# Reordered softmaxes, weight loads and first FFN tiles in a float32 gated cross-attention block on one core

## The chip, the cores and the metric

The kernel runs on one core of a Trainium2 chip. The metric is the device time of one execution in microseconds; lower is better. Three runs of the kernel before gave 1563.82, 1565.23 and 1566.9 us; their median is 1565.23 us.

## The reference

For 32 sequences of 64 tokens of width 512 the kernel computes a cross-attention with 32 heads of width 128 and then a linear layer with a low-rank adapter, both added to the tokens through a gate:

```python
x = x + jnp.tanh(g_xattn[0]) * xattn(_layernorm(x), ctx, mask, bias, Wq, Wk, Wv, Wo)
x = x + jnp.tanh(g_ffn[0]) * ffn(_layernorm(x), weight, bias, lora_A, lora_B, starts)

# xattn: per head
score = einsum('bqhd,bkhd->bhqk', q, k) / sqrt(128) + position_bias    # masked keys: -inf
ctx = einsum('bhqk,bkhd->bqhd', softmax(score), v)                      # then ctx @ Wo
# ffn
y = x @ weight.T + bias + lora(x)
```

All data are float32. Products of the projections are made from operands that are split into a high and a low part, three matmuls for one.

## The kernel before, in words

**Halves and pairs.** The 2048 tokens are worked through in two halves of 1024 (index p). A half has two stages. Stage A (function stage_a) projects the context to keys and values and writes them to device memory. Then the function attention goes through the 32 heads as 16 pairs (n from 0 to 15). The second half ends with the FFN of all tokens, in four chunks of 512 tokens (c from 0 to 3) of four tiles (t).

**One pair.** q_unit(n) makes the queries of a pair with seven products of split blocks (line 352; the block weights are named p1 to p7). score(n) makes the scores, and on VectorE (DVE) adds the bias and takes the maximum (lines 775 and 777); GpSimd (POOL) subtracts it (778), ScalarE (ACT) takes the exponential (787, for pair 0 783). The generator normed sums the row on DVE and multiplies by the reciprocal on POOL (797 to 800). Then the probabilities must be turned: a DVE transpose in 32 x 32 blocks writes a tile tp (811), and eight small ACT copies for each head place its blocks into the tile pts that the value products read (808). pv(n) multiplies by the values (891), in four PSUM groups of two heads i and two column halves c, and splits the result into ch on ACT and cl on DVE (894, 895). oproj(n) multiplies these with the pair's output weights, eight tiles of tokens, and adds each to acc on DVE (925). The weights of queries and of the output come raw from device memory (fetch, line 259), are split by eight steps of prep (305) or two of prep_o (906), on ACT and POOL, and are used then.

**What sets the order.** Each engine executes its instructions in the order in which the Python code issues them. Side work is written as generators in the list streams. beat() (64) advances each of them by one step and is called after every product of a unit, every score, every value group and every output tile. drain(g) runs a generator to its end at once. So the order on ACT, DVE, POOL and SyncE's queue of DMAs (SP) is that of streams at each beat. The sequence of the pairs is written out by hand in run (939). Pairs 0 and 1 go singly, then the loop of line 1005 takes two pairs a pass, from a = 4 to 14, and lines 1020 to 1035 end the half.

**Around the change.** Pair 0's softmax is both(normed(0), first_turned()): row sums of both heads first, then head 0 turned through tp and eight ACT copies, and head 1 turned by eight small DVE transposes right into pts. Pairs 14 and 15 are last_turned() (847): sums and products of pair 14, then, head by head, those of pair 15 and the turn of pair 14, then the turns of pair 15 beside copies, two memsets of a second tile of probabilities, and the rest of the copies. Raw query weights are fetched into one buffer, r0: at the start of odd query units, and after a drain of the even ones' split (lines 998 and 1006). The values of a pair have one buffer (res[3]) of 1 MB, so v of pair 15 is loaded when pv(14) has ended. start_o(14), the split of output 14's weights, begins in line 1024. In the second half the stream ffn_weights (1078) first splits the FFN weights and then normalizes the first four tiles of tokens (ffn_norm); the four transposes and splits of these (ffn_tile, lines 1104 to 1109) stand between the first four tiles of output 13 (between, 1209), and fill (1214) then runs chunk 0 of the FFN. In the first half, fill makes a part of the second half's first keys. ffn_lora(c) is the first user of a chunk's split tiles.

Of the kernel before, what the change touches and what calls it, by code (L numbers as in the profile page):

```python
# [9 lines left out]
F32 = mybir.dt.float32  # L10
# [7 lines left out]
P = 128  # L18
# [25 lines left out]
def flamingo_block(ctx: ExitStack, tc: tile.TileContext, x, xT, ctxT, bias, mask, gx, gf,  # L44
# [257 lines left out]
    PREP = (("s3", "hp1"), ("s2", "lp1", "hp7"), ("s1", "lp7", "hp6"), ("s4", "lp6", "hp5"),  # L302
            ("lp5", "hp2"), ("lp2", "hp4"), ("lp4", "hp3"), ("lp3",))

    def prep(kind, n, eng, wait=0, at=0):
        for _ in range(wait if at == 0 else 0):
            yield
        do = pair_blocks(kind, n, eng)
        for k, ops in enumerate(PREP):
            if at and k == at:  # L310
                for _ in range(wait):
                    yield
            do(*ops)
            yield

    def prep_plain(n, eng, only=None):
# [394 lines left out]
    def attention(p, res, rest):  # L711
# [6 lines left out]
        def load_v(n):  # L718
            b["v", n] = big(res[3], [P, NT, 256], F32, f"v{p}_{n}")
            nc.sync.dma_start(out=b["v", n], in_=vd[p][n // 2][:, :, n % 2 * 256:(n % 2 + 1) * 256])  # L720

        def load_bias(n):
            for i in range(2):
# [31 lines left out]
        def enter_late():  # L755
            nonlocal acc_t, ch, cl
            ch = big(rest[0], [P, 2, TP], F32R, f"ch{p}")
            cl = big(rest[1], [P, 2, TP], F32R, f"cl{p}")
            acc_t = [big(res[5 + i], [P, 4, 512], F32, f"acc{p}_{i}") for i in range(2)]
            acc.extend(acc_t[t // 4][:, t % 4, :] for t in range(NT))  # L760
            fetch("o", p * NPR, "r1")
            for t in range(NT):
                nc.sync.dma_start(out=acc[t], in_=x[p * NT + t])

        acc_t = sm = ch = cl = None
        acc, pts = [], []
# [62 lines left out]
                yield  # L829


        def first_turned():
            n = 0
            tp = rows.tile([P, NT, S], F32, tag="row", name=f"tp{p}_{n}")
            turn(tp, n, 0)
            yield
            for k, q in enumerate(quads):
                copy(nc.scalar.copy, n, 0, tp, *q)
                copy(nc.vector.transpose, n, 1, sm[0][:, 1], *q)
                if k % 3 == 2:  # L840
                    yield
            load_bias(2)
            b["m", 2] = bias_mask(2)
            streams.append(b["m", 2])


        def last_turned():
            n = NPR - 2
            z = kqp.tile([P, 2, NT, S], F32, tag="kq", name=f"tz{p}")
            tp = [rows.tile([P, NT, S], F32, tag="row", name=f"tp{p}_{n}_{i}") for i in range(2)]  # L850
            pts.append(big(res[1], [P, 2, NT, P], F32, f"pz{p}"))
            yield from normed(n, 0)
            for i, _ in enumerate(normed(n + 1, 0)):
                turn(tp[i], n, i)
                yield
            todo = [(n, i, q) for i in range(2) for q in quads]

            def copies(k):
                for m, i, q in todo[:k]:
                    copy(nc.scalar.copy, m, i, tp[i] if m == n else z[:, i], *q)  # L860
                del todo[:k]

            for i in range(2):
                turn(z[:, i], n + 1, i)
                copies(3)
                yield
            for h in range(2):
                nc.vector.memset(pts[1][h * S:(h + 1) * S, :, :, (1 - h) * S:(2 - h) * S], 0.0)
                copies(3)
                yield  # L870
            copies(4)

            def rest():
                todo.extend((n + 1, i, q) for i in range(2) for q in quads)
                while todo:
                    copies(4)
                    yield
            b["s", n + 1] = rest()
            streams.append(b["s", n + 1])
# [4 lines left out]

        def pv(n, cs=(0, 1)):
            drain(b["s", n])
            for c in cs:
                for i in range(2):
                    ps = psum(f"po{p}_{n}_{i}_{c}")
                    for t in range(4):  # L890
                        nc.tensor.matmul(ps[:, t * P:(t + 1) * P], b["v", n][:, c * 4 + t, i * P:(i + 1) * P],  # L891
                                         pts[n > NPR - 2][:, i, c * 4 + t, :], start=True, stop=True)
                    sl = slice(c * 512, (c + 1) * 512)
                    nc.scalar.copy(ch[:, i, sl], ps)  # L894
                    nc.vector.tensor_tensor(cl[:, i, sl], ps, ch[:, i, sl].bitcast(F32), ALU.subtract)  # L895
                    beat()
# [42 lines left out]
        def run(xq, prefetch, before_last, last_unit, fill, freed, last, between=None):  # L939
            qb = {}  # L940

            def start_q(n, *a):
                qb[n] = prep("q", p * NPR + n, *a)
                streams.append(qb[n])

            def q_unit(n):
                g = p * NPR + n
                drain(qb.get(n))
                if n == 0:
                    start_q(1, nc.vector, 2)  # L950
                elif n == NPR - 1:
                    before_last()
                elif n % 2:
                    fetch("q", g + 1, "r0")
                else:
                    start_q(n + 1, nc.gpsimd)
                qT[n] = kqp.tile([P, 2, TP], F32, tag="kq", name=f"qT{g}")
                end = unit(wt[("q", g)], xq, None, k_dst(qT[n]), f"q{g}", tuple(carry))
                carry.clear()
                end()  # L960
                if n == NPR - 1:
                    last_unit()
                elif n % 2 and n > 1:
                    start_q(n + 1, nc.gpsimd)

            def score(*ns):
                for n in ns:
# [2 lines left out]
                    for i in range(2):  # L970
                        scores(n, i, qT[n], b["k", n])
                for n in ns:
                    if n + 2 < NPR:
                        load_k(n + 2)
                n = ns[0]
                if n == 0:
                    b["s", n] = both(normed(n, 0), first_turned())
# [55 lines left out]
            oproj(n - 1, range(4, NT))  # L1033
            pv(n, (1,))
            last(lambda t: oproj(n, range(t, t + 1)), acc)

# [41 lines left out]
    def ffn_weights(tags):  # L1078
        wf = [big(tags[i], [P, KT, 512], F32R, f"wf{i}") for i in range(2)]
        ffn_w.update(wf=wf, tags=tags)  # L1080
        for kt in range(KT):
            split(ffn_w["raw"][:, kt, :], wf[0][:, kt, :], wf[1][:, kt, :], nc.gpsimd)
            yield
# [9 lines left out]
        ffn_w["xn"] = big(tags[6], [P, 4, D], F32, "xn")  # L1093
        for t in range(4):
            ffn_norm(0, t)
            yield

    def ffn_norm(c, t):
        mv = mv2[:, c * 4:(c + 1) * 4, :]
# [63 lines left out]
    for p in range(NPH):  # L1163
# [39 lines left out]
        else:  # L1203
# [88 lines left out]
```

## Time and profile before

| what | us |
|---|---|
| median of three runs | 1565.23 |
| the profiled execution, its own time | 1568.15 |
| its span, first to last instruction | 1566.4 |
| TensorE matmul (PE) busy in the span | 1531.0 |
| weight load (PEld) | 1287.6 |
| POOL, DVE, ACT busy | 1020.6, 963.9, 724.9 |

The profiled execution's own time is its span and 1.75 us around it. Times in views of the profile count from the span's start. A row of a timeline is: start, length, engine, line, operation, output <- inputs, count, and in brackets the idle time before it and what ended it. A row of waits is: who waited for what: total in us, times, longest. Tiles are named without their buffer numbers: po the value product, pt and pz the turned probabilities, v the values, wo the output weights, rawq the raw query weights, wsq the sums in their split, fa the split FFN tiles, xn the normalized tokens. The two halves' attention runs from about 311 to 754 us and from 1053 to 1514; the FFN's chunk 0 lies inside the second, from 1448 to 1473.

### The profile page before, as it was taken

To read this page: it belongs to the slowest core of one execution; us is meant where nothing else is said; L and a number is where in the kernel's file an instruction comes from. 1 tells how busy PE (TensorE), PEld (TensorE's weight loads), DVE (VectorE), ACT (ScalarE), POOL (GpSimd) and SP (SyncE) were. 2 spreads that over 40 slices of the span, in tenths; PEclk is the share of its full clock that TensorE was granted. 3 is DMA by queue.
4 is the path that set the end of the run, shared out by engine and by line. 5 is a ranking of instruction groups with operands and counts; after the bars stand their busy time and mean duration, and the time that the engine had idled before them with its cause. 6 is when DMAs were issued, how large, how long until landed. Compare 5 with 4: busy or idle time off the path is not lost.

```text
span 1566.4 us, 25095 instructions
## 1 busy us (share of the span) xinstructions
PE 1531.0 (98%) x9000; PEld 1287.6 (82%) x9000; DVE 963.9 (62%) x1609; ACT 724.9 (46%) x1594; POOL 1020.6 (65%) x1128
## 2 busy tenths in 40 slices
PE   9999999999999999998999999999999999999898
PEld 7888888878788888886888888887878888888677
DVE  5665554385576656665686557448556665767664
ACT  6344233444564566456344323344466456645511
POOL 3898478866666666662589757886666666676110
PEclk9999999999999999999999999999999999999999
DMA  5754545474244344431565454547324344434111
GB/s 210 261 194 159 199 163 177 148 293 135 95 148 163 133 177 158 152 109 68 196 245 204 152 186 167 191 148 276 136 94 162 148 139 171 168 143 129 48 34 67
DMA packets 111070, 248.50 MB, mean 159 GB/s; under 512 B 10241, under 2 KB 44033, under 8 KB 106850
## 3 DMA queue, kind: packets, MB, share of 16 engines
q1 hardware_dynamic: 110658, 246.38, 44.3%
q8 instruction: 71, 1.16, 0.3%
q10 hardware_dynamic: 288, 0.52, 0.1%
q14 instruction: 53, 0.43, 0.1%
HBM read 173.45 MB, written 73.42 MB: 158 GB/s over the span
## 4 chain that ended last, share of the span: by engine, by line
PE 87%; POOL 4%; DVE 3%; DMA 2%; issue 2%; ACT 2%; SPq 0%; DVEq 0%; POOLq 0%; ACTq 0%
PE pa L98 18%; PE po L891 7%; PE pzv L98 6%; PE pvv L98 6%; PE pxv L98 6%; PE pzk L98 5%; PE pvk L98 5%; PE pxk L98 5%; PE pxq L98 5%; PE pzq L98 5%; PE pvq L98 5%; PE ps L773 3%; PE pf L98 3%; PE pyv L98 3%; PE ppk L98 2%; PE pyk L98 2%
## 5 line engine op out<-in xcount | busy, mean ns | idle before, releaser
L98 PE MATMUL pa<-wo,ch 128*128 128x512 f32 x1024 | 320.1, 393 | 2.1 <-POOL wo L90 1.6
L98 PEld LDWEIGHTS pa<-wo,ch 128*128 128x128 f32 x1024 | 190.8, 188 | 43.2 <-POOL wo L90 2.6
L925 DVE TENSOR_TENSOR acc<-pa,acc 128x512 f32<-128x512 f32 x256 | 173.0, 682 | 73.8 <-PE pa L98 73.1
L808 ACT COPY pt<-tp 32x256 f32<-32x256 f32 x464 | 187.2, 403 | 67.4 <-DVE tp L811 56.5
L98 PE MATMUL pa<-wo,cl 128*128 128x512 f32 x512 | 199.8, 390 | 0.0
L731 POOL TENSOR_TENSOR sm<-sm,madd 128x512 f32<-128x512 f32 x60 | 76.9, 1291 | 127.3 <-DMA sm<-bias 127.3
L895 DVE TENSOR_TENSOR cl<-po,ch 128x512 fp32r<-128x512 f32 x128 | 87.4, 691 | 78.5 <-ACT ch L894 78.4
L891 PEld LDWEIGHTS po<-pt,v 128*128 128x128 f32 x960 | 112.3, 192 | 14.9 <-ACT pt L808 12.5
L891 PE MATMUL po<-pt,v 128*128 128x128 f32 x960 | 113.9, 276 | 10.7 <-ACT pt L808 10.7
L98 PEld LDWEIGHTS pa<-wo,cl 128*128 128x128 f32 x512 | 96.2, 188 | 20.3
L800 POOL TENSOR_TENSOR sm<-sm,r 128x512 f32<-128x512 f32 x64 | 67.0, 1048 | 70.4 <-DVE r L799 68.9
L90 POOL TENSOR_TENSOR wo<-rawo,wo 128x512 fp32r<-128x512 f32 x64 | 81.4, 1295 | 46.9 <-ACT wo L89 46.8
L778 POOL TENSOR_TENSOR sm<-sm,mx 128x512 f32<-128x512 f32 x64 | 67.2, 1050 | 63.0 <-DVE mx L777 63.0
L894 ACT CAST ch<-po 128x512 fp32r<-128x512 f32 x128 | 74.7, 590 | 60.1 <-PE po L891 58.3
L354 DVE TENSOR_TENSOR vt<-pvv,vt 128x512 f32<-128x512 f32 x64 | 44.1, 689 | 93.6 <-PE pvv L98 93.5
L354 DVE TENSOR_TENSOR qT<-pvq,qT 128x512 f32<-128x512 f32 x64 | 44.2, 690 | 69.3 <-PE pvq L98 69.1
L354 DVE TENSOR_TENSOR kT<-pvk,kT 128x512 f32<-128x512 f32 x56 | 38.5, 688 | 67.0 <-PE pvk L98 67.0
L376 ACT COPY vt<-pxv 128x512 f32<-128x512 f32 x32 | 18.9, 589 | 130.9 <-PE pxv L98 130.9
L787 ACT ACTIVATE sm<-sm 128x512 f32<-128x512 f32 x60 | 38.0, 633 | 64.7 <-POOL sm L778 64.7
L354 DVE TENSOR_TENSOR qT<-pzq,qT 128x512 f32<-128x512 f32 x64 | 44.2, 690 | 36.7 <-PE pzq L98 36.4
L773 PE MATMUL ps<-kB,qT 128*64 128x64 f32 x2048 | 64.1, 223 | 0.3 <-DVE qT L354 0.3
L773 PEld LDWEIGHTS ps<-kB,qT 128*64 128x64 f32 x2048 | 61.3, 138 | 3.7 <-issue 1.4
(984 smaller groups left out, 3737.1 us busy)
## 6 DMA issues: line engine op xcount, KB each, us to landing
kd<-kT SPq DMA_DIRECT2D x64, 512.0 KB, 3.4
vd<-vt SPq DMA_DIRECT2D x128, 256.0 KB, 2.3
kB<-kd SPq DMA_DIRECT2D x32, 1024.0 KB, 9.8
v<-vd SPq DMA_DIRECT2D x32, 1024.0 KB, 7.9
rawq<-wq SPq DMA_DIRECT2D x32, 512.0 KB, 8.7
sm<-bias SPq DMA_DIRECT2D x64, 256.0 KB, 7.0
rawo<-wo SPq DMA_DIRECT2D x32, 512.0 KB, 3.6
rawk<-wk SPq DMA_DIRECT2D x31, 512.0 KB, 5.4
```

The source lines that it names most:

```text
L90: eng.tensor_tensor(lo, raw, hi.bitcast(F32), ALU.subtract)
L98: nc.tensor.matmul(ps, a, b, start=start and i == 0, stop=stop and i == 3 * n - 1, skip_group_check=True)
L354: nc.vector.tensor_tensor(o, ps, i, ALU.add)
L731: nc.gpsimd.tensor_tensor(t, t, masks[p][0], ALU.add)
L773: nc.tensor.matmul(ps[h * S:(h + 1) * S, t, :], qT[:, i, tok], kT[:, i, tok], start=True, stop=True)
L778: nc.gpsimd.tensor_tensor(s, s, mx.unsqueeze(2).to_broadcast([P, NT, S]), ALU.subtract)
L800: nc.gpsimd.tensor_tensor(t, t, r.unsqueeze(2).to_broadcast([P, NT, S]), ALU.mult)
L808: f(pts[n > NPR - 2][dst, i, :, src], of[src, :, ki * 32:(ki + 1) * 32])
L891: nc.tensor.matmul(ps[:, t * P:(t + 1) * P], b["v", n][:, c * 4 + t, i * P:(i + 1) * P], pts[n > NPR - 2][:, i, c * 4 + t, :], start=True, ...
L894: nc.scalar.copy(ch[:, i, sl], ps)
L895: nc.vector.tensor_tensor(cl[:, i, sl], ps, ch[:, i, sl].bitcast(F32), ALU.subtract)
L925: nc.vector.tensor_tensor(acc[t], ps, acc[t], ALU.add)
```

## The change

- prep takes a function, then, that its last step calls. start_q gives it the fetch of the next pair's raw query weights; the fetches after drains and at the start of odd units go, and so do these drains. Query 2's split starts before pv(0), query 4's with query unit 3, not after it.
- Pair 0's softmax (first_softmax) goes head by head: sum and turn of head 0, then sum and turn of head 1. Head 1 has both ways: its first four blocks by DVE transposes, the other four through a second tp and ACT copies. pv(0) takes both column halves of head 0 first. Output 0's split starts after five products of query unit 1, no longer ahead of them.
- The loads of acc leave two per beat in a stream (load_acc), followed by the keys of pair 2.
- Pairs 14 and 15: pair 14 is turned right after its own products; then come the sums of pair 15, its turns, and the memsets in the rest.
- pv(14) loads v of pair 15 by halves into the same tile, each when its half of pair 14 is used up.
- start_o(14) comes ahead of output 13, and output 14 gives six tiles, not four, ahead of pv(15).
- The FFN stream starts with the four norms; the four FFN tiles stand between the last four tiles of output 12; the first norm of chunk 1 is in fill.

```diff
-    def prep(kind, n, eng, wait=0, at=0):
+    def prep(kind, n, eng, wait=0, at=0, then=None):
...
             do(*ops)
+            if then and k == len(PREP) - 1:
+                then()
             yield
...
+        def load_v(n, t=None, cs=None):
+            b["v", n] = t or big(res[3], [P, NT, 256], F32, f"v{p}_{n}")
+            for sl in [slice(c * 4, c * 4 + 4) for c in cs] if cs else [slice(0, NT)]:
+                nc.sync.dma_start(out=b["v", n][:, sl], in_=vd[p][n // 2][:, sl, n % 2 * 256:(n % 2 + 1) * 256])
...
+        def load_acc():
             for t in range(NT):
                 nc.sync.dma_start(out=acc[t], in_=x[p * NT + t])
+                if t % 2:
+                    yield
+            load_k(2)
...
-        def first_turned():
+        def first_softmax():
             n = 0
+            tp = [rows.tile([P, NT, S], F32, tag="row", name=f"tp{p}_{n}_{i}") for i in range(2)]
+            norm = normed(n, 0)
+            next(norm)
+            yield
+            turn(tp[0], n, 0)
+            yield
+            next(norm)
+            for q in quads[:4]:
+                copy(nc.scalar.copy, n, 0, tp[0], *q)
+            yield
+            for q in quads[4:]:
+                copy(nc.scalar.copy, n, 0, tp[0], *q)
+            turn(tp[1], n, 1)
+            yield
+            for k in (0, 2):
+                for q in quads[k:k + 2]:
+                    copy(nc.vector.transpose, n, 1, sm[0][:, 1], *q)
+                for q in quads[4 + k:6 + k]:
+                    copy(nc.scalar.copy, n, 1, tp[1], *q)
+                yield
...
             yield from normed(n, 0)
-            for i, _ in enumerate(normed(n + 1, 0)):
+            for i in range(2):
                 turn(tp[i], n, i)
                 yield
...
+            for i, _ in enumerate(normed(n + 1, 0)):
+                copies(3)
+                yield
             for i in range(2):
                 turn(z[:, i], n + 1, i)
                 copies(3)
                 yield
-            for h in range(2):
-                nc.vector.memset(pts[1][h * S:(h + 1) * S, :, :, (1 - h) * S:(2 - h) * S], 0.0)
-                copies(3)
-                yield
             copies(4)
 
             def rest():
+                for h in range(2):
+                    nc.vector.memset(pts[1][h * S:(h + 1) * S, :, :, (1 - h) * S:(2 - h) * S], 0.0)
+                    yield
                 todo.extend((n + 1, i, q) for i in range(2) for q in quads)
-                while todo:
-                    copies(4)
+                for k in (2, 2, 1, 1, 3, 3, 3, 1):
+                    copies(k)
                     yield
...
-            for c in cs:
-                for i in range(2):
+            for i, c in [(i, c) for i in range(2) for c in cs] if n == 0 else [(i, c) for c in cs for i in range(2)]:
...
-            if cs[-1] == 1 and n + 1 < NPR:
+            if n == NPR - 2:
+                load_v(n + 1, b["v", n], cs)
+            elif n + 1 < NPR:
                 load_v(n + 1)
...
+            def start_q(n, eng=nc.gpsimd, wait=0):
+                g = p * NPR + n
+                qb[n] = prep("q", g, eng, wait, then=(lambda: fetch("q", g + 1, "r0")) if n + 1 < NPR else None)
...
-                elif n % 2:
-                    fetch("q", g + 1, "r0")
-                else:
-                    start_q(n + 1, nc.gpsimd)
+                elif n % 2 == 0 or n == 3:
+                    start_q(n + 1)
...
+                if n == 1:
+                    start_o(0)
                 end()
...
-                elif n % 2 and n > 1:
-                    start_q(n + 1, nc.gpsimd)
+                elif n % 2 and n > 3:
+                    start_q(n + 1)
...
-            start_o(0)
+            streams.append(load_acc())
             q_unit(1)
+            start_q(2)
             pv(0)
-            start_q(2, nc.gpsimd)
             score(1)
             oproj(0)
-            drain(qb[2])
-            fetch("q", p * NPR + 3, "r0")
             q_unit(2)
...
             for a in range(4, NPR, 2):
-                drain(qb[a])
-                fetch("q", p * NPR + a + 1, "r0")
                 oproj(a - 3)
...
-                oproj(a - 2)
+                oproj(a - 2, beside=between if a == NPR - 2 else None)
...
             n = NPR - 1
-            oproj(n - 2, range(4), between)
+            start_o(n - 1)
+            oproj(n - 2, range(4))
             fill()
             oproj(n - 2, range(4, 6))
-            start_o(n - 1)
             pv(n - 1, (0,))
             oproj(n - 2, range(6, NT))
             pv(n - 1, (1,))
             start_o(n)
-            oproj(n - 1, range(4))
+            oproj(n - 1, range(6))
...
     def ffn_weights(tags):
...
+        ffn_w["xn"] = big(tags[6], [P, 4, D], F32, "xn")
+        for t in range(0, 4, 2):
+            ffn_norm(0, t)
+            ffn_norm(0, t + 1)
+            yield
...
             def between(t):
-                ffn_tile(0, t)
-                if t == 2:
-                    ffn_norm(1, 0)
+                if t > 3:
+                    ffn_tile(0, t - 4)
 
             def fill():
                 drain(weights)
+                ffn_norm(1, 0)
                 ffn_chunk(0, first=False)
```

More of the change, by code (lines that the diff above doesn't have):

```diff
@@ L716, in load_k @@
             nc.sync.dma_start(out=b["k", n], in_=kd[p][n])
-        def load_v(n):
-            b["v", n] = big(res[3], [P, NT, 256], F32, f"v{p}_{n}")
-            nc.sync.dma_start(out=b["v", n], in_=vd[p][n // 2][:, :, n % 2 * 256:(n % 2 + 1) * 256])
+        def load_v(n, t=None, cs=None):
+            b["v", n] = t or big(res[3], [P, NT, 256], F32, f"v{p}_{n}")
+            for sl in [slice(c * 4, c * 4 + 4) for c in cs] if cs else [slice(0, NT)]:
+                nc.sync.dma_start(out=b["v", n][:, sl], in_=vd[p][n // 2][:, sl, n % 2 * 256:(n % 2 + 1) * 256])
         def load_bias(n):
@@ L829, in turned @@
                 yield
-        def first_turned():
+        def first_softmax():
             n = 0
-            tp = rows.tile([P, NT, S], F32, tag="row", name=f"tp{p}_{n}")
-            turn(tp, n, 0)
+            tp = [rows.tile([P, NT, S], F32, tag="row", name=f"tp{p}_{n}_{i}") for i in range(2)]
+            norm = normed(n, 0)
+            next(norm)
             yield
[L837 to L840, printed above, removed]
-                    yield
+            turn(tp[0], n, 0)
[14 more added lines that the diff above has]
+                yield
             load_bias(2)
@@ L866, in last_turned @@
                 yield
-            for h in range(2):
-                nc.vector.memset(pts[1][h * S:(h + 1) * S, :, :, (1 - h) * S:(2 - h) * S], 0.0)
-                copies(3)
-                yield
             copies(4)
             def rest():
+                for h in range(2):
+                    nc.vector.memset(pts[1][h * S:(h + 1) * S, :, :, (1 - h) * S:(2 - h) * S], 0.0)
+                    yield
                 todo.extend((n + 1, i, q) for i in range(2) for q in quads)
-                while todo:
-                    copies(4)
+                for k in (2, 2, 1, 1, 3, 3, 3, 1):
+                    copies(k)
                     yield
@@ L886, in pv @@
             drain(b["s", n])
-            for c in cs:
-                for i in range(2):
[L889 to L896, printed above, removed]
-            if cs[-1] == 1 and n + 1 < NPR:
+            for i, c in [(i, c) for i in range(2) for c in cs] if n == 0 else [(i, c) for c in cs for i in range(2)]:
+                ps = psum(f"po{p}_{n}_{i}_{c}")
+                for t in range(4):
+                    nc.tensor.matmul(ps[:, t * P:(t + 1) * P], b["v", n][:, c * 4 + t, i * P:(i + 1) * P],
+                                     pts[n > NPR - 2][:, i, c * 4 + t, :], start=True, stop=True)
+                sl = slice(c * 512, (c + 1) * 512)
+                nc.scalar.copy(ch[:, i, sl], ps)
+                nc.vector.tensor_tensor(cl[:, i, sl], ps, ch[:, i, sl].bitcast(F32), ALU.subtract)
+                beat()
+            if n == NPR - 2:
+                load_v(n + 1, b["v", n], cs)
+            elif n + 1 < NPR:
                 load_v(n + 1)
@@ L940, in run @@
             qb = {}
-            def start_q(n, *a):
-                qb[n] = prep("q", p * NPR + n, *a)
+            def start_q(n, eng=nc.gpsimd, wait=0):
+                g = p * NPR + n
+                qb[n] = prep("q", g, eng, wait, then=(lambda: fetch("q", g + 1, "r0")) if n + 1 < NPR else None)
                 streams.append(qb[n])
@@ L972, in score @@
                 for n in ns:
-                    if n + 2 < NPR:
+                    if 0 < n < NPR - 2:
                         load_k(n + 2)
@@ L976, in score @@
                 if n == 0:
-                    b["s", n] = both(normed(n, 0), first_turned())
+                    b["s", n] = first_softmax()
                 elif n == NPR - 2:
@@ L1032, in run @@
             pv(n, (0,))
-            oproj(n - 1, range(4, NT))
+            oproj(n - 1, range(6, NT))
             pv(n, (1,))
@@ L1090, in ffn_weights @@
         nc.gpsimd.tensor_tensor(b2[1][0:64, :], br[0:64, :], b2[0][0:64, :].bitcast(F32), ALU.subtract)
+        yield
         nc.scalar.copy(a2[:, :, 0:NL * R], ar)
         nc.gpsimd.tensor_tensor(a2[:, :, 64:64 + NL * R], ar, a2[:, :, 0:NL * R].bitcast(F32), ALU.subtract)
[L1093 to L1096, printed above, removed]
     def ffn_norm(c, t):
```

## The prediction

> **What bounds the kernel now.** I read the page first, then the busy time of four stretches, the waits of TensorE, the chain of waits, and at last the single engines around each wait.
>
> ```profile
> span 1566.4 us, 25095 instructions
> PE 1531.0 (98%) x9000; PEld 1287.6 (82%) x9000; DVE 963.9 (62%) x1609; ACT 724.9 (46%) x1594; POOL 1020.6 (65%) x1128
> ```
> TensorE sets the time, and the diff removes no matmul. All that can be won is TensorE's idle 35.4 us and what it runs slowly after idling. Busy time by stretch (columns: stretch, length, then PE, PEld, DVE, ACT, POOL, granted clock, DMA) shows where that is:
>
> ```profile
> 322.00:412.00 90.00, 84.12 (x632) 70.64 (x631) 59.80 (x108) 45.63 (x105) 62.79 (x73) 1.00 0.46 161
> 694.00:754.00 60.00, 52.94 (x367) 44.60 (x366) 37.62 (x64) 27.74 (x61) 18.15 (x18) 0.97 0.31 106
> 1064.00:1153.00 89.00, 83.10 (x627) 69.78 (x626) 58.79 (x106) 44.77 (x104) 61.68 (x72) 1.00 0.46 163
> 1436.00:1504.00 68.00, 57.33 (x394) 48.21 (x393) 41.24 (x70) 28.79 (x61) 15.25 (x14) 0.92 0.21 69
> ```
> These are the first and last attention pairs of each half; they idle 5.88, 7.06, 5.90 and 10.67 us, 29.5 of the 35.4. The long middle stretches (412 to 694, 754 to 1064, 1153 to 1436) idle 0.00. The waits name the causes:
>
> ```profile
> PE po L891 <- ACT pt L808: 10.7, 7, 2.0
> PE po L891 <- DMA v<-vd: 7.6, 2, 4.0
> PE pt L1117 <- DVE fa L1109: 5.6, 1, 5.6
> PE pvq L98 <- DVE qT L354: 2.4, 2, 1.3
> PE pa L98 <- POOL wo L90: 1.6, 2, 0.8
> ```
> So: probabilities not yet copied (7 times), the last values' load (twice), the FFN's first split tile, a query eviction. Behind them, on ScalarE, GpSimd and in the chain:
>
> ```profile
> 360.49 0.41 ACT L295 CAST wq3p<-rawq 128x256 fp32r<-128x256 f32 x1 [2.44 <-DMA rawq<-wq]
> ```
> ```profile
> 390.39 1.43 POOL L299 TENSOR_TENSOR wq4p<-wsq,wq4p 128x256 fp32r<-128x256 f32 x2
> 391.78 1.43 POOL L299 TENSOR_TENSOR wq4p<-rawq,wq4p 128x256 fp32r<-128x256 f32 x2
> 393.17 0.74 POOL L299 TENSOR_TENSOR wq4p<-wsq,wq4p 128x256 fp32r<-128x256 f32 x1
> 393.87 2.05 POOL L800 TENSOR_TENSOR sm<-sm,r 128x512 f32<-128x512 f32 x2
> ```
> ```profile
> 723.87 8.28 DMA v<-vd
> 1484.55 7.94 DMA v<-vd
> ```
> A cast of raw query weights waits for their load and holds the probability copies queued behind it; the drained split of query 4 stands ahead of the softmax's products; the last values' load is on the path itself.
>
> **What the Trainium skill says.** "PSUM — Partial Sum Buffer", section "Engine vs sequencer instructions": ScalarE's, VectorE's and GpSimd's queues are strictly first in, first out. The trace agrees: copies that were ready at 358.0 start at 360.80, behind the cast that idled 2.44. "TensorE: Matmul & The Clock Gate", section "What's actually happening": after an idle window of about 3.4 us the clock is halved. The trace agrees: after the 3.98 us wait 16 value matmuls took 3.65 against 1.95 elsewhere; after 1.80 us, 24 took 2.94, hardly longer. "DMA: Bandwidth & Descriptors", section "Measured (HBM→SBUF, 128 partitions, SWDGE, issued from GpSimd)": 1 MB in 6.15 us, issued from GpSimd. Here, from SyncE, it takes 8.28, and that is used.
>
> **The change part by part.** Times are on the before trace's clock.
>
> *First softmax, pair 0.* Before, head 0's turn (332.75) stands behind both row sums, though GpSimd had its product at 330.64. Now it follows at 331.0 to 331.7; eight copies of 0.42 and one eviction of 0.58 end at 335.0; TensorE is free at 335.9. Head 0's 16 matmuls, now first, run to 337.65. Head 1: product on GpSimd to 334.5, turn to 335.2, then four direct turns on DVE (4 x 0.44, two additions of 0.69 between) to 337.55 and four ScalarE copies to 337.3. The 1.50 wait goes. Price: the output weights' casts move from 330.2 to 337.3, their two GpSimd splits (1.30) to 337.9 to 340.5, and query 2's split now starts in pv(0). ScalarE's third eviction then stands behind a cast that needs GpSimd at 341.2, so the low part that output 0 needs is there at 342.9 and TensorE at 342.6: 0.3 lost. The eight acc loads (0.33 each) now leave over four beats, behind query 2's; they land near 336, and output 0, their first reader at 343, covers them up to 7 us.
>
> *Pair 1.* GpSimd from 340.5: seven query steps (0.73) to 345.6, subtraction 1.05, mask 1.29, step 0.73, subtraction 1.05, mask 1.29, three steps 2.2, to 353.1; two products to 355.2 (before 354.90). Nothing won there, but query 3 is asked for when query 2's last reader ends at 352.5, not at 356.32: with the same 4.14 us it lands at 356.7, not 360.46. ScalarE from the turn at 354.8: 16 copies (6.8), two evictions (1.2), four casts (1.6) come to 364.4 with nothing to wait for. TensorE is there at 363.4 (unit of 9.5 and a 0.2 wait for an eviction from 352.8, plus 0.9): 1.0 us instead of 1.80.
>
> *Raw query weights, query 4.* Before, its load (374.43) queues behind wo and v, and its steps block GpSimd to 393.91. Now it is asked for near 367.9, lands near 372, and is split in query unit 3, where GpSimd idled from 373.36 to 381.69. The turn at 394.94 comes near 389. Late next are ScalarE's copies, with the 3 us of lead that pairs 6 and up have without a wait; so 1.27 and 1.14 go. The new wait on SyncE ends with GpSimd's last reader of the old raw weights; behind it queue wo, v, k and bias. Value loads have slack (issued 414.43, landed 421.56, used 430.43), so nil. Half 0: 5.71 - 0.3 - 0.2 - 1.0 = **4.2**; half 1 (1.48, 1.97, 1.11, 1.18): **4.2**.
>
> *Last softmax, output 14's weights, values by halves.* Pair 14's turns no longer stand behind pair 15's sums: 705.2 instead of 706.22. Output 14's splits start with output 13 (raw landed 699.55), so ScalarE has two casts earlier (1.2); 16 copies end at 713.8 and TensorE asks at 713.05: 0.75 instead of 1.65. The two weight waits (0.57, 0.85) go: split done by 707.8; output 15's load follows at once and lands near 711 instead of 726.64. GpSimd's 2.6 us of splits push pair 14's second product to 706.5, which the copies' queue hides. The first half of v15 is asked for when half of pv(14) is done (714.8), used at 727.4 (output 14 now gives six tiles ahead, not four); the second 719.2 and 731.9. The trace has no 512 KB v load: bounds are 3.1 (shortest raw query load) and 8.28 (the whole), I take 4.5, and slack is 12.6, so nil at both ends; output 14's tiles are the cover, and without them the whole 4.5 less 1.8 for each half shows. The two memsets (0.91) go behind the copies into output 13 and pv(14), where DVE idled; the last copies end near 725. Work from 709.44 to 742.96 is 12 output tiles of 1.36 and 8 value groups of 0.89, 23.4 us in 33.5: 10.1 too many, of which 0.75 and 0.2 for slow starts stay: **9.1**. Half 1, 1473.32 to 1503.29, 30.0 against 23.4: 6.5, 0.1 stays: **6.4**.
>
> *FFN tiles in output 12.* Norms (4 x 0.6) and split tiles (0.59 ACT, 0.65 DVE each) go where DVE does one 0.69 addition per 1.36 us; GpSimd's weight splits follow them and still end near 1435. From 1432.98 to 1458.77, the first FFN product, now: 1.88 for the transposes moved ahead, pv 3.67, scores 3.88, four tiles 5.5, lora 1.82: it is at 1449.8. But the next chunk's first norm is in fill, behind DVE's backlog of pair 14: four score steps to 1445.4, two of 1.71, two of 1.3, the norm 0.53: 1451.95. So a new wait of 2.2 on that norm takes the place of 0.68 and 5.63, short of halving the clock. The FFN product starts at 1452.7 with 0.3 for the start after it: 1458.77 - 1453.0 = **5.8**.
>
> Sum 4.2 + 4.2 + 9.1 + 6.4 + 5.8 = 29.7. The profiled execution took 1568.15 (span 1566.4 and 1.75 around it), so 1538.45; the median of the runs lies 2.92 lower: **1535.5**.
>
> **Rivals.** *The queues move the wait (1543).* GpSimd is full from 337.9 to 355.2 by my list; if DVE and GpSimd hinder each other there, pair 1 keeps its wait and query 4's split eats its lead: 2 per half instead of 4.2, and the FFN norm's backlog grows by 3: 7.4 less, 1543. For: "SBUF — State Buffer", section "SBUF: two separate sides", says that a DVE operation with two SBUF inputs and a GpSimd one lock each other out of a shared port pair; the trace agrees, a 0.41 us split on DVE took 1.51 at 318.04 beside GpSimd's, and my sum has no such delay. Also, GpSimd's second product comes no earlier. Against: most idle there is for data. *The halves are taken for one tile (1547).* If values by halves wait for each other, pv(14)'s second half waits for the first load: 719.3 against 717.4, 2 us, and the last load lands after use, 4 more, in each half: 12 less. Against: the two halves of a bias tile are issued apart (353.97 and 355.67), each after its own turn. *Slower (1571).* SyncE is one queue, and the query loads now stand ahead of v and wo. In six passes per half a v load has 430.43 - 421.56 = 8.9 us to spare. If GpSimd's last reader delayed it by 11.9, each pass would lose 3.0, 12 passes 36, more than the 29.7: 1571. It decides from 11.4 on. Against: GpSimd's split ends 3 us before the wo fetch that blocks SyncE today.
>
> **How the numbers follow.** Forecast 0.56; first rival 0.24; second 0.10; slower 0.04; 0.06 for better than the sum (all 36 us of idle and slow matmuls won: 1529). The range, 1531 to 1546, leaves out the slower case, most of the second rival and the best. About 0.2%, 3 us, is what a measurement of this kernel can tell from no change: faster 0.94, same 0.02, slower 0.04.
>
> **What would show it.** Right: no wait on v, none on the query eviction, none of wo in output 14; copies' waits of about 1 us left at pair 1; 2 us on the FFN norm; query loads issued ahead of wo and v; the clock of the last stretches near 1. Wrong: waits on copies of 2 us at pairs 0 to 2, any on v, or idle in the middle stretches, which now have none.

## Result and the profile after

The changed kernel takes 1536.83 us, the median of five runs (1536.32 to 1539.37), against 1565.43 before (five runs, 1563.82 to 1566.9). The ratio is 0.982, with a 95% interval of 0.9806 to 0.9834: 28.6 us faster. The forecast was 1535.5.

The profiled execution took 1536.32. Its page (span; then busy time, share and count by engine):

```profile
span 1534.5 us, 25110 instructions
PE 1521.8 (99%) x9000; PEld 1283.6 (84%) x9000; DVE 964.9 (63%) x1603; ACT 728.3 (47%) x1602; POOL 1020.2 (66%) x1128
```

No engine has less to do. Only TensorE is busy 9.2 us less, at the same 9000 matmuls: mostly matmuls that ran slowly around idle time, 5.6 us of it at a lowered clock (an estimate from the starts of the matmuls in both traces). Its idle time fell from 35.4 to 12.7 us. The busy time of the four stretches that idled before (start and end, length, then PE, PEld, DVE, ACT, POOL, clock, DMA):

```profile
322.00:405.00 83.00, 81.76 (x625) 69.42 (x624) 56.76 (x103) 46.35 (x106) 63.53 (x73) 1.00 0.50 175
692.00:740.00 48.00, 46.45 (x259) 39.53 (x254) 35.28 (x59) 26.77 (x58) 15.94 (x16) 1.00 0.36 125
1051.00:1134.00 83.00, 81.74 (x625) 69.41 (x624) 57.72 (x103) 46.46 (x106) 64.05 (x74) 1.00 0.50 175
1424.00:1483.00 59.00, 56.49 (x290) 47.71 (x289) 44.48 (x75) 25.07 (x53) 14.56 (x25) 1.00 0.20 67
```

They idle 1.24, 1.55, 1.26 and 2.51 us, 6.6 in place of 29.5, and the clock is 1.00 in all. TensorE's waits in the attention (total, times, longest):

```profile
PE po L912 <- ACT pt L816: 3.1, 3, 1.5
PE tpf L137 <- DVE xn L132: 2.5, 1, 2.5
PE po L912 <- DVE pt L816: 0.6, 2, 0.3
```

The waits on v, on the output weights and on the query eviction are gone. Copies are waited for at pair 1 (0.76 and 0.82) and at pair 14 of half 0 (1.54), and the new wait on chunk 1's first norm is there.

To place the gain, both traces were cut at the first matmul of certain units, so that each difference belongs to one step. Traces differ by up to 2.2 us ahead of query unit 1, where none of the changed work lies; the steps leave that out.

| step | predicted | measured |
|---|---|---|
| start of half 0 (query units 1 to 5) | 4.2 | 5.35 |
| tail of half 0 | 9.1 | 8.27 |
| start of half 1 (query units 17 to 21) | 4.2 | 5.38 |
| FFN tiles, to the first FFN product | 5.8 | 5.95 |
| tail of half 1 | 6.4 | 6.55 |
| the rest (before query unit 1, chunk 0, the end) | 0 | 0.35 |
| sum | 29.7 | 31.85 |

Every step is within 1.2 us of its number; the starts of the halves gained 1.2 us more than forecast each. All are measured from one trace of the kernel before; how far the tails stand for its usual run is taken up below. The experiments ask, part by part, whether these numbers are right for the reasons that the prediction gave.

### The profile page after: what moved, and what is told of

It is laid out like the page before. It is cut to its first block, busy times and chain, and to the rows that moved or that the text cites. A ratio compares the mean times of both kernels' runs of the same rounds, so it can differ in the third digit from the quotient of the medians.

```text
span 1534.5 us, 25110 instructions
## 1 busy us (share of the span) xinstructions
PE 1521.8 (99%) x9000; PEld 1283.6 (84%) x9000; DVE 964.9 (63%) x1603; ACT 728.3 (47%) x1602; POOL 1020.2 (66%) x1128
## 3 DMA queue, kind: packets, MB, share of 16 engines
q8 instruction: 71, 1.16, 0.3%
## 4 chain that ended last, share of the span: by engine, by line
PE 93%; DVE 3%; ACT 2%; POOL 1%; issue 1%; DMA 0%; DVEq 0%; ACTq 0%; POOLq 0%
PE pa L98 21%; PE po L912 7%; PE pzv L98 6%; PE pvv L98 6%; PE pxv L98 6%; PE pxq L98 5%; PE pzq L98 5%; PE pvq L98 5%; PE pzk L98 5%; PE pvk L98 5%; PE pxk L98 5%; PE ps L781 4%; PE pyv L98 3%; PE pf L98 3%; PE ppk L98 2%; PE pyq L98 2%
## 5 line engine op out<-in xcount | busy, mean ns | idle before, releaser
L816 ACT COPY pt<-tp 32x256 f32<-32x256 f32 x472 | 190.4, 403 | 66.2 <-DVE tp L819 55.1
```

Of the source, the lines that this page charges most:

```text
L816: f(pts[n > NPR - 2][dst, i, :, src], of[src, :, ki * 32:(ki + 1) * 32])
```

## The experiments

Three groups of four; each group ran on one chip beside the kernel before, whose median was 1562.32, 1564.01 and 1566.74 there. Ratios are to it. Gains "in the trace" go from mark to mark as above.

| kernel | median us | ratio, 95% interval |
|---|---|---|
| after, v whole, six tiles | 1537.25 | 0.9837 (0.9821 to 0.9853) |
| after, v halves, four tiles | 1538.06 | 0.9844 (0.9829 to 0.9859) |
| after, v whole, four tiles | 1539.85 | 0.9855 (0.9841 to 0.9870) |
| before, v halves | 1556.30 | 0.9959 (0.9944 to 0.9974) |
| after, old first softmax | 1538.43 | 0.9838 (0.9823 to 0.9853) |
| after, old query fetches | 1550.68 | 0.9918 (0.9901 to 0.9936) |
| before, output 14's split early | 1558.57 | 0.9961 (0.9951 to 0.9971) |
| before, FFN part | 1561.42 | 0.9986 (0.9976 to 0.9996) |
| after once more | 1538.45 | 0.9822 (0.9809 to 0.9836) |
| after, old last softmax | 1544.87 | 0.9863 (0.9849 to 0.9876) |
| after, norm and split moved | 1534.57 | 0.9797 (0.9784 to 0.9811) |
| after, all four moves | 1532.17 | 0.9782 (0.9769 to 0.9795) |

**The last values: halves or tiles?** Three kernels undo one or both (the first part of the edit loads v whole, the second gives four tiles):

```diff
-            if n == NPR - 2:
-                load_v(n + 1, b["v", n], cs)
-            elif n + 1 < NPR:
+            if cs[-1] == 1 and n + 1 < NPR:
...
-            oproj(n - 1, range(6))
+            oproj(n - 1, range(4))
```

> The changed kernel, but the last values are loaded whole again after pv(14); output 14 still gives six tiles ahead of pv(15). My theory (six tiles alone cover nearly all of a whole load): issued near 714.7 the load of 8.3 us lands near 723.0, wanted at 722.72, so a wait of 0.3 to 0.8 us in half 0 and 0 to 0.5 in half 1; 0.3 to 1.3 us slower in all. Rival (the halves are what gained): the wait is back, 8 to 11 us slower.

> The changed kernel with values by halves, but output 14 gives four tiles ahead of pv(15) again. My theory (the halves land 6 us before use, so two tiles fewer don't show on v): no wait on v in either half; at most 1 us a half on pair 15's last copies, which are now wanted 2.7 us sooner (they end near 721.0 beside a use at 720.0); 0 to 2 us slower in all. Rival (the six tiles are what covers the load): 3 to 4 us a half, 6 to 8 in all.

> The changed kernel with both undone: last values whole after pv(14), four tiles of output 14 ahead of pv(15). My theory (either cover is enough by itself, so only both together matter): load lands near 723, wanted at 720.0: a wait on v of 3.0 to 3.5 us in each half, and 0.5 to 1.7 us of slow matmuls after it; 7 to 10 us slower in all, far more than the sum of the two single undoings. Rival (each has a share of its own, which add): the time is the sum of the two single undoings.

With v whole nothing was lost in either tail: the load took 5.85 and 5.78 us, not 8.28, and landed 2.1 us ahead of use. Four tiles cost 0.3 in each half. Both together cost 1.1 and 0.7 (the rest of this kernel's time is mostly slow matmuls in chunk 0, see below). The waits in its tails, as the view names them:

```profile
PE po L912 <- ACT pz L816: 0.9, 1, 0.9
PE po L912 <- ACT wo L89: 0.4, 1, 0.4
```

The view names ScalarE, but the load of v came last. It landed at 721.27 and 1465.73, and TensorE starts 0.14 us later both times, as after both waits on v in the kernel before (landed at 732.15, started at 732.28). In half 1 the last copy into pz only begins as TensorE starts:

```profile
1465.87 2.02 PE L912 MATMUL po<-pz,v 128*128 128x128 f32 x16 [0.45 <-ACT wo L89]
```

```profile
1465.86 0.40 ACT L816 COPY pz<-tz 32x256 f32<-32x256 f32 x1
```

The two undoings do more than add (1.8 against 0.6 in the trace), through the wait that the theory named, but at a quarter of its size: the load took 6.15 and 5.74 us, not 8.3. So neither the halves nor the tiles carry the 14.8 us of the two tails. Next, the kernel before with nothing but load_v by halves and its call in pv(14):

> The kernel before, with only the loading of the last values by halves put in. My theory: the two waits on v (3.98 and 3.64 us) and the slow value matmuls after them (3.65 us for 16 in place of 1.95, so 1.7 each) go, nothing takes their place, since pair 15's copies were done early there: 10 to 11 us faster. Rival (the load was late together with something else, copies or the output weights, that shows next): 4 to 6 us faster.

No wait on v is left in it. Its two tails gain 5.9 and 5.5 us, 11.4 in the trace, a little over what was expected, but by medians it is only 6.0 faster, the rival's size. The medians of before lie up to 6 us below its profiled execution, so a gain measured from that one trace is larger than that of the usual run. The halves take the wait away in the kernel before, and are worth nearly nothing in the kernel after: something else in the change does the same.

**Output 14's split.** The last value products of pair 14 in the kernel before, and SyncE's DMA issues after them:

```profile
718.62 1.95 PE L891 MATMUL po<-pt,v 128*128 128x128 f32 x16
```

```profile
723.45 0.33 SPq L264 DMA_DIRECT2D rawo<-wo  x1
723.87 0.52 SPq L720 DMA_DIRECT2D v<-vd  x1
```

The products end at 720.57, and with them the last use of pair 14's values. The load of v leaves 3.3 us later (2.05 in half 1), behind a fetch that waits for GpSimd's split of output 14's weights (ended 723.42). In all eleven traces in which that fetch leaves early, the load (or its second half) leaves 0.03 us after the products. One line moved in the kernel before takes that away:

```diff
+            start_o(n - 1)
             oproj(n - 2, range(4), between)
             fill()
             oproj(n - 2, range(4, 6))
-            start_o(n - 1)
```

> The kernel before, with one line moved: the split of output 14's weights starts ahead of output 13. Values whole, four tiles. New theory, after the runs on the halves: what made the last value load late was that it stood in SyncE's queue behind the fetch of output 15's weights, which waited for that split, and then shared the DMA engines with it (8.28 us; 5.8 alone). Then the three waits on the weights go, v is asked for at the end of pv(14) (721.6), lands near 727.4, wanted at 726.9, and no slow matmuls follow: 6.0 to 6.6 us before the second half, 4.5 to 5 in the second, about 11 in the trace and, as the median of before lies below its trace, 6 to 11 by medians. Rival (only smaller loads or more tiles ahead help, the load takes 8 us anyway): 3 to 5 us, with a wait of 2 to 3 on v left in each half.

```profile
708.51 0.34 SPq L264 DMA_DIRECT2D rawo<-wo  x1
724.33 0.52 SPq L720 DMA_DIRECT2D v<-vd  x1
```

```profile
PE po L891 <- ACT pt L808: 11.1, 8, 2.7
PE pt L1117 <- DVE fa L1109: 6.3, 1, 6.3
...
PE po L891 <- DMA v<-vd: 0.6, 1, 0.6
```

The fetch now leaves 16 us ahead of v, and the load takes 5.95 and 6.04 us. Of 7.6 us of waits on v, 1.4 are left: the view names v for 0.64; the 0.76 in half 1 that it puts down to an addition on DVE (acc) also ends 0.14 after v landed. The tails gain 4.1 and 5.5 in the trace; in half 0 pv(14) waits 2.73 for copies, not 1.65, and slow matmuls follow. By medians the kernel is 5.4 us faster (6 to 11 were expected), where the halves alone gave 6.0: moving this one line does nearly what the halves do. (That the fetch ahead lengthens v's load is not shown: behind the same fetch, in the kernel with the FFN part alone, v took 6.2 and 6.7 us, against 8.28 and 7.94 in the kernel before.)

**The old first softmax.** The whole of first_softmax is replaced by both(normed(0, 0), first_turned()), and pv(0) goes by column halves:

> The changed kernel with pair 0's old softmax (both row sums first, head 1 wholly by DVE transposes) and pv(0) column half by column half. My theory: the wait of pv(0) on the turned probabilities is 1.5 us again in place of 0.3, and nothing later takes it up, so query unit 2 starts 1.2 to 1.4 us later than in the changed kernel, in each half; 2.4 to 2.8 in all, and pair 1's wait of 0.8 stays. Rival (pair 0's delay is slack for pair 1, so that its wait shrinks by as much): 0.5 to 1 us in all.

```profile
PE po L900 <- ACT pt L816: 4.6, 3, 1.6
```

pv(0) waits 1.51 and 1.49 again (the third of these waits is pair 14's), and query units 2 and 18 start 1.16 and 1.22 us later. But the waits of pair 1 vanish, and units 3 and 19 are only 0.13 later. The rival's mechanism holds, at less than its size: pair 1's copies are ready at a time that TensorE's earlier coming doesn't move. The total, 2.7 us more in the trace, looks like the theory's and isn't: 1.6 of it are slow matmuls in chunk 0 (below), and 0.9 came before query unit 1.

**The old query fetches.** start_q, q_unit and the drains in run are those of before; start_o(0) stays in its new place:

> The changed kernel with the old places of the query weights' fetches, drains and splits (query 3 and the even ones fetched after a drain, odd ones in the unit, query 2's split after pv(0), query 4's after query unit 3). My theory: the loads of query 3 and 4 are late again, with waits of about 1.8 at pv(1), 1.2 at the query eviction and 1.1 at pv(2): 1.0 us at query unit 3 and 3.0 at query unit 5, 4.0 in each half, 8 in all. Rival (GpSimd's order in the softmax, not the loads, set these waits): under 3 us in all.

```profile
PE po L912 <- ACT pt L816: 9.4, 5, 3.0
...
PE pvq L98 <- DVE qT L356: 1.5, 2, 0.8
```

ScalarE ahead of pv(1) (start, length, in brackets the idle time and what ended it):

```profile
359.78 0.41 ACT L295 CAST wq3p<-rawq 128x256 fp32r<-128x256 f32 x1 [1.59 <-DMA rawq<-wq]
...
364.09 0.40 ACT L295 CAST wq3p<-wsq 128x256 fp32r<-128x256 f32 x1 [0.64 <-POOL wsq L288]
```

The fetch of query 3 leaves at 356.46, not 351.80, and a cast with copies behind it waits 1.59 for it and 0.64 for the sums. pv(1) waits 2.54 and 2.99 (expected 1.8), at least in part because TensorE comes to it 1.5 us earlier than in the kernel before; and after these waits, matmuls are slow. TensorE by stretch (busy, clock):

```profile
363.00:366.00 3.00, 0.46 (x4) 1.00 0.00 0
366.00:370.00 4.00, 4.00 (x22) 0.57 0.02 4
370.00:374.00 4.00, 4.00 (x21) 1.00 0.09 11
```

Pair 1 loses 3.4 and 3.7, pair 2 2.5 and 2.5: 6 in each half, where 4 was expected; by medians the kernel is 12 to 14 us slower than the kernel after, the largest loss of the parts undone. Without the early fetches the starts of the halves are 0.4 and 0.7 slower than in the kernel before, though the new first softmax is in place.

**The FFN part alone.** ffn_weights, between and fill as after, in the kernel before:

> The kernel before, with only the FFN part of the change (norms first in the FFN stream, the four tiles in output 12, chunk 1's first norm in fill). My theory: the waits of 0.68 and 5.63 go, one of 2 to 2.5 on the norm comes, and the slow matmuls of chunk 0 (1.7) go in those executions in which 2.5 us of idling don't lower the clock: the first FFN product 4.0 to 4.5 us sooner, the end of chunk 0 4.5 to 6.2; the tail's wait on v of 3.6 stays. Rival (the norms in output 12 push DVE's work on outputs and scores back): less than 3 us, with waits in output 12 or pv(13).

```profile
PE po L891 <- DMA v<-vd: 4.3, 2, 2.4
PE tpf L137 <- DVE xn L132: 4.2, 1, 4.2
```

The first FFN product comes 4.2 sooner, but the norm is waited for 4.2, not 2.5, with slow matmuls behind it: at the end of chunk 0 3.0 are left, the rival's size. By medians it is 2.6 us faster. The place of the tiles is right, but DVE is behind.

This trace also shows how much of the tails' gain is one execution. Its tails are those of the kernel before, and v left as late (3.3 and 2.07 us after the products), yet they took 3.7 and 1.3 us less: v landed after 6.16 and 6.67 us, with waits of 1.87 and 2.39 in place of 3.98 and 3.64. Against this execution the tails of the kernel after gain 4.5 and 5.3, the halves alone 2.2 and 4.3, the early split alone 0.4 and 4.3.

**The old last softmax.** In the kernel after, last_turned is that of before; all else stays:

> The changed kernel with the old order of the last softmax (pair 15's sums ahead of pair 14's turns, memsets ahead of the last copies); the early split of output 14's weights, the halves and the six tiles stay. My theory, from the kernel before with only the early split (pv(14) waited 2.73) and with only the FFN part (the norm was waited for 4.18): the new order is what makes room on DVE for both. Wait of pv(14) in half 0 1.55 to 2.7 with 1.6 of slow matmuls, wait on the norm in half 1 2.5 to 4.2 with 1.6 of slow matmuls: 4.5 to 6 us slower. Rival (the prediction's price, 0.9 a half for the pair's own turns): under 2 us.

```profile
PE tpf L137 <- DVE xn L132: 5.7, 1, 5.7
PE po L910 <- ACT pt L816: 4.6, 4, 2.7
```

6.4 us slower than the kernel after by medians beside it, and 7.1 in the traces from query unit 1 on, more than expected. The wait on the norm is 5.67: with the old order pair 15's sums, too, stand ahead of it on DVE, between the turns of pair 14, and two of their small multiplies take 1.00 and 0.90 (see the last experiment but one). In half 0, pv(14) waits 2.73, this time without slow matmuls after it.

**The clock after a wait of 2.5 us.** The kernel after once more:

> The changed kernel as it is, as the measure for the three beside it. Theory of the clock (an idle window of about 2.4 to 2.5 us is where the granted clock begins to fall, so the wait on chunk 1's first norm is followed by slow matmuls in some executions and not in others, at 1.6 us): the runs lie in two groups about 1.6 us apart, near 1536.4 and 1538.1. Rival (the wait never slows TensorE and the spread is common noise): one group, within 0.6 us.

These four runs lie at 1538.06 to 1538.75: one group, the upper, so this measurement alone does not decide. The first one had 1536.32, 1536.46, 1536.83, 1537.10, and 1539.37. With v whole and six tiles there were two of each, 1536.38 and 1536.40, 1538.10 and 1538.14. The trace of one of these upper ones (1538.10), then that of the kernel after, in chunk 0 (stretch, length, busy, clock, DMA):

```profile
1430.00:1434.00 4.00, 1.48 (x9) 0.99 0.07 12
1434.00:1438.00 4.00, 4.00 (x12) 0.58 0.34 121
1438.00:1442.00 4.00, 4.00 (x21) 1.00 0.17 66
```

```profile
1430.00:1434.00 4.00, 1.49 (x10) 1.00 0.14 35
1434.00:1438.00 4.00, 4.00 (x21) 1.00 0.25 98
1438.00:1442.00 4.00, 4.00 (x22) 1.00 0.19 70
```

The same wait of 2.51 us, then 12 matmuls in four microseconds or 21. So the rival falls: the same wait lowers the clock in one execution and not in another. Over all traces here: after waits up to 1.97 us the clock didn't fall; of twelve waits from 2.39 to 2.99, nine came with a lowered clock; of seven from 3.64 up, all. Between 1.97 and 2.39 no wait is on record. In chunk 0 a fall costs 1.6 us.

**Norm and split moved.** Two moves in the kernel after:

```diff
             def between(t):
                 if t > 3:
                     ffn_tile(0, t - 4)
+                if t == NT - 1:
+                    streams.append(early())
+
+            def early():
+                yield
+                ffn_norm(1, 0)
...
                 drain(weights)
-                ffn_norm(1, 0)
...
-            start_o(n - 1)
+            start_o(n - 1, 1)
```

The second argument delays the split's first step by one beat.

> The changed kernel with two moves: chunk 1's first norm goes into pv(13), ahead of the last softmax, and the split of output 14's weights starts one beat later, so that GpSimd's subtractions no longer lie beside DVE's small multiply (1.00 us there, 0.17 elsewhere). My theory: the multiply takes 0.17 again, pair 14's second turn comes 0.8 sooner and pv(14) in half 0 waits 0.7 in place of 1.55; in half 1 the wait of 2.5 on the norm goes, with its slow matmuls, and at most 0.6 comes back as a wait on the adapter's operands: 2.7 to 3.3 us faster than the changed kernel's fast group, 3 to 5 by medians. Rival (DVE's backlog as a whole sets chunk 0's start, not the norm's place in it): the wait moves to the adapter or the tiles, under 1 us.

DVE in the kernel after, at the sums of pair 14, and GpSimd beside it:

```profile
697.11 0.17 DVE L807 TENSOR_TENSOR r<-r,rv 128x8 f32<-128x8 f32 x1
...
698.74 1.00 DVE L807 TENSOR_TENSOR r<-r,rv 128x8 f32<-128x8 f32 x1
...
701.46 0.68 DVE L819 STREAM_TRANSPOSE tp<-sm 128x512 f32<-128x512 f32 x1
```

```profile
698.42 1.29 POOL L90 TENSOR_TENSOR wo<-rawo,wo 128x512 fp32r<-128x512 f32 x1
```

The small multiply has two inputs in SBUF and ends as GpSimd's subtraction does (699.74 and 699.71). With the split a beat later:

```profile
698.86 0.17 DVE L807 TENSOR_TENSOR r<-r,rv 128x8 f32<-128x8 f32 x1
...
700.74 0.69 DVE L819 STREAM_TRANSPOSE tp<-sm 128x512 f32<-128x512 f32 x1
```

The second turn comes 0.72 sooner, and pv(14) waits 0.73, not 1.55. In half 1 the 2.5 us and the slow matmuls after them are gone; 0.99 comes back at the second tile, whose norm follows the first tile's split on DVE (the expectation had 0.6, on the adapter). It is 3.9 us faster than the kernel after on the same chip, whose runs all lay in the upper group. Against the lower one it is 2.2 faster in the traces, where 2.7 to 3.3 were expected.

**All four moves.** Besides these two, output 13 ends ahead of pv(14), and at pair 1 DVE copies four of the sixteen blocks:

```diff
-            oproj(n - 2, range(4, 6))
+            oproj(n - 2, range(4, NT))
             pv(n - 1, (0,))
-            oproj(n - 2, range(6, NT))
...
-                    copy(nc.scalar.copy, n, i, tp[i], *q)
+                    copy(nc.vector.tensor_copy if (i, q) in onv else nc.scalar.copy, n, i, tp[i], *q)
```

> The two moves of the kernel beside it, and two more: output 13 ends ahead of pv(14) (2.7 us more cover for pair 14's copies), and at pair 1 four of the sixteen copies of turned probabilities go to DVE. My theory: the waits of pv(14) go wholly, pair 1's 0.8 us in each half goes, as ScalarE has 1.7 us less to copy; 5 to 7 us faster than the changed kernel, near 1531. Rival (DVE's copies delay its evictions of the query unit as much as they help ScalarE): only the 3 to 5 us of the kernel beside it, plus 0.7 in half 0.

```profile
PE tpf L137 <- DVE xn L132: 1.0, 1, 1.0
PE po L912 <- DVE pt L816: 0.7, 2, 0.3
```

No wait on ScalarE's copies is left. 1532.17 us is 6.3 less than the kernel after in the same group of four (5 to 7 were expected), about 1.6 of it the fall of the clock there, and the fastest of all; the intervals of the two ratios (0.9769 to 0.9795, 0.9809 to 0.9836) lie apart.

## Why the prediction was right, and where it was not

**The total** is right in part by luck, as two errors cancel. The sum was 2.1 too small: 1538.45 for the profiled execution, which took 1536.32. Then 2.92 were taken off because before's trace lay above its median; that doesn't carry over. After's trace lies 0.5 below its median. What put before's execution above its median is seen only in part: its tails took 3.7 and 1.3 us more than those of another execution, with longer loads of v and longer waits on them.

**First softmax (1.2 a half by its terms, the wait of 1.50 less 0.3 left).** The wait went as worked out, even to the 0.3 left. But as a part of its own it is worth 0.13 a half: pair 1 gives the rest back. The step "Nothing won there" on GpSimd at pair 1 had this in it; the sum did not draw the conclusion.

**Query weights (0.6 at pair 1 and 2.4 at pair 2).** Mechanism right: query 3 landed at 355.08 (predicted 356.7), pv(1) waits 0.76 in place of 1.0, and pair 2's waits are gone. The steps gained 1.0 and 1.1 at pair 1 and 3.0 and 2.9 at pair 2, more than priced; why is not shown. Undone, the part costs 6 a half, as longer waits at pair 1 lower the clock.

**Last values.** The wait on v went, as forecast, but the halves were not what it took. "The trace has no 512 KB v load", so 4.5 us were assumed; the halves took 3.5 to 3.7. "Output 14's tiles are the cover": with four in place of six, 0.3 a half is lost; no run takes them all away. The prediction looked at the load's length and not at its place in SyncE's queue, 3.3 us behind the fetch for output 15. It had that fetch landing "near 711 instead of 726.64" and did not draw from it that v then leaves at once. It priced the early split at the waits on the weights (0.57 and 0.85 in half 0); alone in the kernel before it is worth 5.4 by medians, both halves together. The early split and the halves each remove the wait on v, so their gains don't add.

**Last softmax.** "0.75 instead of 1.65" at pv(14): 1.54. The step "GpSimd's 2.6 us of splits push pair 14's second product to 706.5, which the copies' queue hides" missed DVE's multiply beside them, 1.00 for 0.17: with the split a beat later the wait is 0.73. The part itself was under-priced: undone, it costs 1.7 in half 0 and 5.5 by the end of chunk 0 in half 1, since the FFN tiles' gain rests on it.

**FFN tiles.** 5.8 and a wait of 2.2; measured 5.95 and 2.5, of which the same multiply (0.99 at 1429.06) delayed DVE by 0.8. "Short of halving the clock" held in the trace of the kernel after and failed in other executions: "TensorE: Matmul & The Clock Gate", section "What's actually happening", gives a window of about 3.4 us, and here the clock fell with seven of nine waits of 2.39 to 2.54. The measurement decides.

**The rivals.** Queues that move the wait: the lock of "SBUF — State Buffer", section "SBUF: two separate sides", is real here, at 0.8 a time and not 7.4. Halves treated as one tile: no, they leave at 710.19 and 714.74. SyncE slower: no wait on v in any pass.

**Open:** why v whole took 8.28 and 7.94 in the trace of before and 5.7 to 6.7 in the experiments' tails, and what decides whether a wait of 2.5 us lowers the clock. No run takes the early split or the FFN tiles out of the kernel after, so their worth there is inferred from the kernel before.

## What to carry to other kernels

Before a late load is split or covered, look at what stands ahead of it in its queue: here one early split of weights gained 5.4 us by medians, and halving the load 6.0. Parts that remove the same wait don't add, and a part's worth alone says little: taking the new first softmax out costs 0.1 a half, and the FFN tiles gain half without the new last softmax. A step measured from one trace holds for that execution; a second trace of the same code can move it by 3.7 us. Price a wait with what follows it: from 2.4 us of idle TensorE on, more often than not 1.6 us more.

## What was not expected of the hardware

The granted clock fell with waits from 2.39 us on, not in each execution, to 0.50 to 0.64 over four microseconds; a wait of 2.73 us at the same place lowered it in one kernel and not in another. A 128 x 8 multiply on DVE took 1.00 us in place of 0.17 beside a 128 x 512 subtraction on GpSimd, 0.8 us that a profile counts as busy.
